# A conditioned transformer block on one core: moving a softmax division to another slot, and spreading the softmax maxima in 32-column tiles

## The chip, the core and the metric

The kernel runs on one core of one Trainium2 chip. A core has TensorE (PE in the profile; PEld is its weight load), VectorE (DVE), ScalarE (ACT), GpSimd (POOL) and SyncE (SP, which here only issues DMAs). The metric is device time in microseconds (us): of the kernel before, 2452.37 us as the median of three runs (2448.12 to 2452.83). Times of single instructions come from one profiled execution.

## What is computed

x is [4, 1024, 512] and t is [4, 128], both f32. The block is added to x once more at the end.

```python
def _tc_rmsnorm(x, t, gw, gb, bw, bb):
    g = (t @ gw.T + gb)[:, None, :]
    b = (t @ bw.T + bb)[:, None, :]
    inv_rms = jax.lax.rsqrt(jnp.mean(x * x, axis=-1, keepdims=True) + EPS)
    return g * x * inv_rms + b

def _attention(x, Wq, Wk, Wv, Wo):          # 16 heads of 32
    attn = jnp.einsum('blhd,bmhd->bhlm', q, k) / scale
    p = jax.nn.softmax(attn, axis=-1)
    o = jnp.einsum('bhlm,bmhd->blhd', p, v).reshape(B, L, D)
    return o @ Wo.T

def _swiglu(x, gate_w, hid_w, out_w):       # hidden width 2048
    return jax.nn.silu(x @ gate_w.T) * (x @ hid_w.T) @ out_w.T

y = x + _attention(_tc_rmsnorm(x, t, g1w, g1b, b1w, b1b), Wq, Wk, Wv, Wo)
return x + y + _swiglu(_tc_rmsnorm(y, t, g2w, g2b, b2w, b2b), gate_w, hid_w, out_w)
```

## The kernel before

**Tiling.** Features lie on the partitions. The 4096 tokens form 8 blocks of 512. Attention is cut into units j: one block, four heads, 256 queries; there are 64 of them. A unit takes four rounds g, each with 256 of the 1024 keys, so there are 256 rounds of attention. Four rounds from a multiple of 4 are called a group here, and the rounds in it slot 0 to slot 3 (in the code: kind = g % 4). Eight groups are the 32 rounds of a block; "position 12" means the group whose first round has g % 32 = 12.

**A round.** Round g multiplies the scores of its keys (`scores`, L310), copies them from PSUM to SBUF (`keep`, L317, on ACT) and takes a running maximum on DVE (`running_max`, L322 and L325). After the fourth round of a unit the maximum is taken over the keys: eight PE transposes (`max_T`, L331, in slot 0), then DVE (`parts`, L337 to L342), which writes each negated maximum as three bf16 numbers whose sum is the f32 value: 4 heads by 3 parts, 12 columns of a 128-column tile `split`. In slot 1, `parts_T` transposes these on PE into 12 rows (L347) and ACT copies them to `mT` (L349); `spread` multiplies `mT` with 0/1 weights `select` (L357), which adds the three parts and repeats the sum on all 128 partitions, two heads at a time; ACT copies the result to `shift` (L358). Then, five rounds after its scores, a tile gets its maximum subtracted on DVE (`shifted`, L363) and goes through the exponential on ACT (`exponential`, L366). One round later `weighted` multiplies it with v on PE (av, L376), and a DMA from POOL adds it to the unit's running sum (`accumulate`, L390). When a unit is through, DVE folds the sum in two (`fold_sum`, L398, slot 0), PE sums it over the keys (`sums`, L408), ACT copies that (L413), DVE takes the reciprocal (`inverse`, L416) and multiplies it with the copied av (`normalize`, L425) into oT. The last two are the division that the change moves. oT is read by the output projection of the block, more than a group later.

**What lies around it.** In the opening, rounds 0 to 59, PE also projects keys, queries and values of all batches from a queue of chains. From round FS = 60 on, the feed-forward part of earlier blocks fills PE: each pair of rounds handles one 128-wide slice p of the hidden layer, by a scheme that shares products (pa and pb, in eighths called pair_15 to pair_7), with DVE steps L546 (`sub_5`), L524 (`add_15`, which pa<-x,fa of the next even round needs), L561 (`gate`), L564 (`hidden`), and the contraction pc, which DVE adds to the result (`take_contract`, L577). Norms are spread over fixed rounds too: L632 (a reciprocal of 128x512) and L193 (scaling) for the next batch in the opening; L138, L193, L491 to L497 at positions 8 to 28 of a block later.

**Order.** The order of instructions on PE, DVE, ACT and POOL is the order of the code, written out by hand; semaphores come from the tile framework. So an instruction that waits holds up everything behind it on its engine. Helper `mm` (L103) splits a matmul into pieces of columns[0] output rows: 32 (four pieces, each on its own 32 columns of PE's array, shown as 128*32) in nearly all work, 128 in parts of the opening and at its start. Forms as 128*32 give the rows times the columns of the array that an instruction uses. PSUM tiles of tag "w" come from two banks that pc, pt, both sp and pa take in turn.

Of the kernel before, what the change touches and what calls it, by code (L numbers as in the profile page):

```python
# [11 lines left out]
BF16 = mybir.dt.bfloat16  # L12
# [5 lines left out]
P = 128  # L18
# [6 lines left out]
def tile_cond_transformer_block(  # L25
# [13 lines left out]
    nc = tc.nc  # L39
# [7 lines left out]
    DH = D // N_HEADS  # L47
    HG = P // DH
    FG = 4
    HQ = 256  # L50
# [6 lines left out]
    const = ctx.enter_context(tc.tile_pool(name="const", bufs=1))  # L57
    sb = ctx.enter_context(tc.tile_pool(name="sb", bufs=1))
# [8 lines left out]
    ident_bf = const.tile([P, P], BF16, tag="ident_bf", name="ident_bf")  # L67
# [8 lines left out]
    NP = 3 * HG  # L76
    split = [const.tile([P, QT, P], BF16, tag=f"split{i}", name=f"split{i}") for i in range(2)]
# [2 lines left out]

    pick = const.tile([NP, HG], F32, tag="pick", name="pick")
    nc.vector.tensor_reduce(pick, ident[:NP, :NP].rearrange("p (h i) -> p h i", i=3), AX.X, ALU.add)
    select = const.tile([NP, HG, P], BF16, tag="select", name="select")
    nc.vector.tensor_copy(select, pick.unsqueeze(2).to_broadcast([NP, HG, P]))
    mod = const.tile([P, 4 * C, B], F32, tag="mod", name="mod")

    condT = const.tile([P, B], F32, tag="condT", name="condT")
# [15 lines left out]
    def mm(dst, w, moving, start: bool, stop: bool, seeded: bool = False):  # L103
        n = columns[0]
        for k in range(0, P, n):
            nc.tensor.matmul(  # L106
                dst[k : k + n, :], w[:, k : k + n], moving, start=start, stop=stop, skip_group_check=seeded
            )

    y, wkq, wv, wo, kq, v = {}, {}, {}, {}, {}, {}  # L110
    raw, rmax, shift, mT, av, acc, avs, oT = {}, {}, {}, {}, {}, {}, {}, {}
# [232 lines left out]
    def parts_T(j: int):  # L344
        pt = ps.tile([P, HQ // P, P], BF16, tag="w", name=f"pt{j}")
        for qt in range(HQ // P):
            nc.tensor.transpose(pt[:, qt, :], split[j % 2][:, qt, :], ident_bf)  # L347
        mT[j] = sb.tile([NP, HQ], BF16, tag="mT", name=f"mT{j}", bufs=2)
        nc.scalar.copy(mT[j], pt[:NP, :, :].rearrange("p a b -> p (a b)"))  # L349

    def spread(j: int, k: int):

        if k == 0:
            shift[j] = sb.tile([P, HG, HQ], F32, tag="shift", name=f"shift{j}")
        pp = ps.tile([P, 2, HQ], F32, tag="w", name=f"sp{j}_{k}")
        for i in range(2):
            nc.tensor.matmul(pp[:, i, :], select[:, k + i, :], mT[j], start=True, stop=True)  # L357
        nc.scalar.copy(shift[j][:, k : k + 2, :], pp)  # L358

    def shifted(r: int, heads: slice = slice(0, HG)):  # L360
# [54 lines left out]
    def inverse(j: int):  # L415
        nc.vector.reciprocal(state["total", j], state["total", j])  # L416

    def normalize(j: int):

        m, qh = divmod(j, NB // HQ)  # L420
        n, hg = divmod(m, C)
        total = state.pop(("total", j))
        if (n, hg) not in oT:
            oT[n, hg] = sb.tile([P, NB], F32, tag=f"oT{hg}", name=f"oT{m}")
        nc.vector.tensor_tensor(oT[n, hg][:, qh * HQ : (qh + 1) * HQ], avs.pop(j), total, ALU.mult)  # L425
# [157 lines left out]
    GB = C * (NB // HQ)  # L583
    BS = GB * UN
# [38 lines left out]
    for b in range(1, B):  # L623
        for half in range(QB):
            s = math.ceil((len(queue) + 1) / PACE)
            s4 = s - 4 - (s - 6) % UN
            tag = f"a{b}_{half}"
# [10 lines left out]
    FS = BS + 28  # L638
# [3 lines left out]
    for n in range(NBLK):  # L642
# [7 lines left out]
        if n < NBLK - 1:  # L650
            tag = f"f{n}"
# [46 lines left out]
    with tc.manual_schedule(  # L698
# [35 lines left out]
        direct = NR // UN - 2  # L734
        late = None
        g = 0
# [31 lines left out]
        while g < END:  # L768
            kind = g % UN
# [6 lines left out]
            j_n = g // UN - 3  # L776
            n_on = 0 <= j_n < NR // UN
            ffn = g >= FS
            p = (g - FS) // 2
# [3 lines left out]
            if kind == 1 and m_on:  # L783
                parts_T(j_m)
            if g < NR:
                scores(g)
            if kind == 1 and m_on:
                spread(j_m, 0)
# [14 lines left out]
            if kind == 1 and m_on:  # L803
                spread(j_m, 2)
                mT.pop(j_m)
                shifted(r_x, slice(0, HG // 2))
                shifted(r_x, slice(HG // 2, HG))
# [54 lines left out]
            else:  # L862
# [34 lines left out]
                    chain(g)()  # L897
                for fn, a in halfway.pop(g, []):
                    fn(*a)
            if kind == 0 and n_on and j_n < direct:  # L900
                inverse(j_n)

                if j_n != GB:
                    normalize(j_n)
            columns[0] = DH
            for fn, a in ended.pop(g, []):
                fn(*a)
# [93 lines left out]
```

## Time and profile before

| What | us |
|---|---|
| median of three runs | 2452.37 |
| the profiled execution, in all | 2447.08 |
| its span, first to last instruction | 2445.3 |
| PE / DVE / ACT / POOL busy | 2386.7 / 1938.9 / 1416.2 / 172.8 |
| 256 exponentials, mean of one (L366) | 1.915 |
| 256 score copies, mean of one (L317) | 1.873 |
| 192 shifts in one piece, mean of one (L363) | 2.282 |
| 64 reciprocals of a division (L416) | 1.744 |
| 64 products of a division (L425) | 0.425 |
| 256 spread matmuls (L357) | 0.270 |
| 128 transposes of the parts (L347) | 0.219 |

Busy time counts an engine's instructions, not what it waited for; matmuls overlap, so their single durations can't be added. The opening takes the first 540 us, the rounds with feed-forward work run to about 2125 us, the feed-forward rest to the end. A line of the timeline gives the start in us from the span's start, the time in us (of several instructions merged, from the first's start to the last's end), engine, line, operation, what it writes and reads, the form, the count, and in brackets the idle time before it and what ended that. A line of the waits gives who waited for whom, the total in us, the number and the longest. A line of windows gives the stretch, its length, busy time and count of PE, PEld, DVE, ACT and POOL, then the granted PE clock (1.00 is full), the DMA engines' busy share and GB/s.

### The profile page before, as it was taken

To read this page: it belongs to the slowest core of one execution; us is meant where nothing else is said; L and a number is where in the kernel's file an instruction comes from. 1 tells how busy PE (TensorE), PEld (TensorE's weight loads), DVE (VectorE), ACT (ScalarE), POOL (GpSimd) and SP (SyncE) were. 2 spreads that over 40 slices of the span, in tenths; PEclk is the share of its full clock that TensorE was granted. 3 is DMA by queue.
4 is the path that set the end of the run, shared out by engine and by line. 5 is a ranking of instruction groups with operands and counts; after the bars stand their busy time and mean duration, and the time that the engine had idled before them with its cause. 6 is when DMAs were issued, how large, how long until landed. Compare 5 with 4: busy or idle time off the path is not lost. (4 is left out here: it accounts for less than half of the span.)

```text
span 2445.3 us, 71149 instructions
## 1 busy us (share of the span) xinstructions
PE 2386.7 (98%) x31785; PEld 1128.7 (46%) x31785; DVE 1938.9 (79%) x2180; ACT 1416.2 (58%) x1495; POOL 172.8 (7%) x207
## 2 busy tenths in 40 slices
PE   8999999999999999999999999999999999999999
PEld 3333333334445544545454544454455445444544
DVE  2688888878889988999799979997999889843332
ACT  3677777666566655666566656665666566512110
POOL 0000000000000000000000000000000000000000
PEclk9999999999999999999999999999999999999999
DMA  6599999988888988889788988888888888853442
GB/s 214 168 284 253 250 256 235 232 205 216 206 201 208 220 224 197 208 215 234 195 208 208 237 206 197 209 226 211 206 205 206 226 200 205 212 165 118 143 129 71
DMA packets 185983, 501.70 MB, mean 205 GB/s; under 512 B 21319, under 2 KB 78663, under 8 KB 158286
## 3 DMA queue, kind: packets, MB, share of 16 engines
q0 software_dynamic: 28656, 208.68, 44.2%
q1 hardware_dynamic: 156734, 288.47, 35.5%
q8 instruction: 250, 4.10, 0.7%
q14 instruction: 55, 0.45, 0.1%
q10 hardware_dynamic: 288, 0.01, 0.0%
HBM read 246.44 MB, written 41.97 MB: 118 GB/s over the span
## 5 line engine op out<-in xcount | busy, mean ns | idle before, releaser
L317 ACT COPY raw<-sc 128x2048 f32<-128x2048 f32 x256 | 479.4, 1873 | 200.1 <-PE sc L310 133.4
L363 DVE TENSOR_TENSOR raw<-raw,shift 128x2048 f32<-128x2048 f32 (+1 forms) x320 | 589.0, 1856 | 3.3 <-ACT shift L358 2.8
L366 ACT ACTIVATE raw<-raw 128x2048 f32<-128x2048 f32 x256 | 490.2, 1915 | 128.9 <-DVE raw L363 124.8
L322 DVE TENSOR_TENSOR rmax<-rmax,raw 128x1024 f32<-128x1024 f32 x384 | 469.5, 1223 | 54.4 <-ACT raw L317 47.9
L106 PE MATMUL pc<-h,ow 128*32 128x512 f32 x4096 | 467.7, 593 | 3.3 <-DMA ow<-in_out_w 2.3
L376 PE MATMUL av<-raw,v 128*32 128x256 f32 x4096 | 275.8, 387 | 34.5 <-ACT raw L366 30.6
L390 POOL DMA_DIRECT2D raw<-raw x192 | 165.7, 863 | 1959.3 <-ACT raw L366 886.0
L310 PE MATMUL sc<-q,k 32*128 32x256 f32 x4096 | 293.3, 400 | 0.3 <-ACT raw L317 0.3
L106 PE MATMUL pa<-x,fa 128*32 128x256 f32 x4096 | 268.2, 379 | 0.3 <-DVE pa L524 0.2
L106 PE MATMUL pa<-sums,fw 128*32 128x256 f32 x4096 | 267.9, 379 | 0.0
L106 PEld LDWEIGHTS pc<-h,ow 128*32 128x32 f32 x4096 | 128.2, 110 | 246.7 <-issue 225.4
L310 PEld LDWEIGHTS sc<-q,k 32*128 32x128 f32 x4096 | 184.9, 184 | 116.6 <-issue 66.6
L106 PE MATMUL pkq<-y,wkq 128*32 128x512 f32 (+1 forms) x1664 | 234.3, 601 | 4.2 <-ACT y L196 4.1
L376 PEld LDWEIGHTS av<-raw,v 128*32 128x32 f32 x4096 | 107.4, 109 | 159.0 <-ACT raw L366 52.2
L106 PEld LDWEIGHTS pa<-x,fa 128*32 128x32 f32 x4096 | 131.1, 110 | 103.0 <-issue 8.8
L106 PEld LDWEIGHTS pa<-sums,fw 128*32 128x32 f32 x4096 | 133.1, 110 | 87.9
L577 DVE SCALAR_TENSOR_TENSOR res<-pc,res 128x512 f32<-128x512 f32 x128 | 88.2, 689 | 76.0 <-PE pc L106 75.0
L556 ACT ACTIVATE t<-pa 128x512 f32<-128x512 f32 x128 | 77.5, 605 | 109.9 <-PE pa L106 109.5
L539 ACT COPY pb<-pa 128x256 f32<-128x256 f32 x128 | 45.9, 359 | 160.3 <-PE pa L106 158.9
L106 PE MATMUL pb<-x,fw 128*32 128x256 f32 x2048 | 134.0, 379 | 1.2 <-ACT pb L539 1.2
L106 PE MATMUL pa<-x,fw 128*32 128x256 f32 x2048 | 135.2, 381 | 0.0
L106 PEld LDWEIGHTS pkq<-y,wkq 128*32 128x32 f32 (+1 forms) x1664 | 73.2, 118 | 131.5 <-issue 118.3
(106 smaller groups left out, 2214.4 us busy)
## 6 DMA issues: line engine op xcount, KB each, us to landing
raw<-raw POOLq DMA_DIRECT2D x192, 1024.0 KB, 9.1
fw<-sw SPq DMA_DIRECT2D x128, 512.0 KB, 7.5
fa<-in_gh_w SPq DMA_DIRECT2D x128, 384.0 KB, 6.5
ow<-in_out_w SPq DMA_DIRECT2D x128, 256.0 KB, 3.7
wkq<-in_kq_w SPq DMA_DIRECT2D x32, 512.0 KB, 5.9
v<-vs SPq DMA_DIRECT2D x128, 128.0 KB, 5.5
k<-kqs SPq DMA_DIRECT2D x124, 128.0 KB, 6.8
kqs<-st SPq DMA_DIRECT2D x61, 256.0 KB, 7.4
```

Of the source, the lines that this page charges most:

```text
L106: nc.tensor.matmul(dst[k : k + n, :], w[:, k : k + n], moving, start=start, stop=stop, skip_group_check=seeded)
L310: nc.tensor.matmul(sc[:, i, k, :], keys[rows, k * P : (k + 1) * P], queries[rows, :], start=True, stop=True)
L317: nc.scalar.copy(raw[r].rearrange("p k h q -> p h k q"), state.pop(("sc", r)))
L322: nc.vector.tensor_tensor(rmax[j], rmax[j], raw[r][:, k, :, :], ALU.max)
L363: nc.vector.tensor_tensor(t, t, s.unsqueeze(1).to_broadcast(list(t.shape)), ALU.add)
L366: nc.scalar.activation(raw[r], raw[r], AF.Exp)
L376: nc.tensor.matmul(av[j][i * DH : (i + 1) * DH, :], v[m, u][:, k, i * DH : (i + 1) * DH], raw[r][:, k, i, :], start=(kt == 0), stop=(kt == ...
L390: nc.gpsimd.dma_start(out=acc[j].rearrange("p k h q -> p (k h q)"), in_=raw[r].rearrange("p k h q -> p (k h q)"), accum_op=ALU.add,)
L539: nc.scalar.copy(bank_b[p][:, RIGHT], bank_a[p][:, RIGHT])
L556: nc.scalar.activation(state["t", p], bank_a[p], AF.Tanh, scale=0.5)
L577: nc.vector.scalar_tensor_tensor(r, pp, 0.5, r, ALU.mult, ALU.add)
```

## The change

Two parts. The first is in the spread: `select` gets 128 rows instead of 12 (the others zero), `mT` becomes two constant tiles of 128 rows, zeroed once and of which the copy writes the first 12; the transposes take 32 columns of `split` instead of 128, and the spread goes through `mm`. Since columns[0] is 32 there, each of the four spread matmuls of a unit becomes four of 32 columns. The sums are the same, with zeros added.

The second moves the division (L416, L425) of most units. Before, it is the last DVE work of slot 0 but for the work listed to come after a round. Now it stays there only for the last unit of each block, and from round 60 on for positions 0, 4, 8, 16 and 20; at positions 12, 24 and 28 and in the opening it comes at the same place in slot 2, two rounds later. The conditions on j_n == GB and direct are as before.

```diff
-    select = const.tile([NP, HG, P], BF16, tag="select", name="select")
-    nc.vector.tensor_copy(select, pick.unsqueeze(2).to_broadcast([NP, HG, P]))
+    select = const.tile([P, HG, P], BF16, tag="select", name="select")
+    nc.vector.memset(select, 0.0)
+    nc.vector.tensor_copy(select[:NP], pick.unsqueeze(2).to_broadcast([NP, HG, P]))
+    parts_of = [const.tile([P, HQ], BF16, tag=f"mT{i}", name=f"mT{i}") for i in range(2)]
+    for t in parts_of:
+        nc.vector.memset(t, 0.0)
...
-            nc.tensor.transpose(pt[:, qt, :], split[j % 2][:, qt, :], ident_bf)
-        mT[j] = sb.tile([NP, HQ], BF16, tag="mT", name=f"mT{j}", bufs=2)
-        nc.scalar.copy(mT[j], pt[:NP, :, :].rearrange("p a b -> p (a b)"))
+            nc.tensor.transpose(pt[:DH, qt, :], split[j % 2][:, qt, :DH], ident_bf)
+        mT[j] = parts_of[j % 2]
+        nc.scalar.copy(mT[j][:NP], pt[:NP, :, :].rearrange("p a b -> p (a b)"))
...
-            nc.tensor.matmul(pp[:, i, :], select[:, k + i, :], mT[j], start=True, stop=True)
+            mm(pp[:, i, :], select[:, k + i, :], mT[j], True, True)
...
-            if kind == 0 and n_on and j_n < direct:
-                inverse(j_n)
-
-                if j_n != GB:
-                    normalize(j_n)
+            if n_on and j_n < direct and kind in (0, 2):
+
+
+                at = g - kind
+                in_first = j_n % GB == GB - 1 or (at >= FS and at % BS not in (12, 24, 28))
+                if in_first == (kind == 0):
+                    inverse(j_n)
+
+                    if j_n != GB:
+                        normalize(j_n)
```

## The prediction

> **What bounds the kernel now.** I read the page's shares of busy time, then the list of waits, then the timeline of one ordinary group of four rounds, of one opening group and of one group with norm work.
>
> ```profile
> PE 2386.7 (98%) x31785; PEld 1128.7 (46%) x31785; DVE 1938.9 (79%) x2180; ACT 1416.2 (58%) x1495; POOL 172.8 (7%) x207
> ...
> PE av L376 <- ACT raw L366: 30.6, 24, 3.5
> ...
> 1516.30 1.05 PE L106 MATMUL pb<-x,fw 128*32 128x256 f32 x16
> ...
> 1517.27 0.12 PEld L347 LDWEIGHTS <-split 128*128 128x128 bf16 x2 [0.41 <-DVE res L577]
> 1517.29 0.27 PE L347 MATMUL pt<-ident_bf,split 128*128 128x128 bf16 x2
> 1517.49 1.15 PE L310 MATMUL sc<-q,k 32*128 32x256 f32 x16
> 1518.46 0.38 PE L357 MATMUL sp<-mT,select 12*128 12x256 bf16 x2
> 1518.77 1.07 PE L376 MATMUL av<-raw,v 128*32 128x256 f32 x16
> 1519.77 0.39 PE L357 MATMUL sp<-mT,select 12*128 12x256 bf16 x2
> 1520.09 1.07 PE L106 MATMUL pa<-x,fw 128*32 128x256 f32 x16
> 1520.20 0.59 ACT L358 COPY shift<-sp 128x512 f32<-128x512 f32 x1 [0.68 <-PE sp L357]
> 1520.68 1.88 ACT L317 COPY raw<-sc 128x2048 f32<-128x2048 f32 x1
> 1522.44 0.39 ACT L402 COPY avs<-av 128x256 f32<-128x256 f32 x1
> 1522.70 1.94 ACT L366 ACTIVATE raw<-raw 128x2048 f32<-128x2048 f32 x1
> 1523.68 1.15 PE L310 MATMUL sc<-q,k 32*128 32x256 f32 x16
> ```
>
> PE is the bound. Where it stops, it waits almost always for one thing: in slot 2 of a group, av waits for an exponential, whose shift DVE did late. Adding up the timeline's gaps before av, about 17.5 us of the 30.6 lie in the opening (rounds 6 to 59) and nearly all the rest in later groups, 1.28 us at position 16 and 0.67 at position 24 of each 32-round block. (Position 12 waits 0.55, put down to another ACT copy behind the same exponential.) In the ordinary group shown no wait is reported, but there is little room: the exponential ends at 1524.64 and av starts at 1524.76. Its chain is spread copy, score copy, avs copy, exponential: ACT, without a gap, not DVE.
>
> **What the Trainium skill says.** "TensorEngine Tiling (Array Packing)", section Key Properties: changing the tiling mode drains the array, changing the tile inside a mode doesn't. The trace agrees: av to its 128*32 successor takes 0.89 us from start to start, av to the 12*128 spread 1.00. The same page, Gotcha 2, says that column tiling excludes fast weight load; no row here shows bf16 in column tiles. "TensorE: Matmul & The Clock Gate", Part 1: an idle array falls to half clock and needs about 3.4 us of work to recover. The trace shows three such falls, after the stalls at 160, 227 and 361 us:
>
> ```profile
> 160.00:164.00 4.00, 3.87 (x32) 1.42 (x36) 3.97 (x4) 3.56 (x4) 0.00 (x0) 0.65 0.94 219
> 227.00:231.00 4.00, 4.00 (x32) 1.26 (x28) 3.94 (x7) 2.01 (x2) 0.00 (x0) 0.59 0.98 289
> 361.00:366.00 5.00, 4.95 (x40) 1.67 (x44) 4.97 (x5) 4.16 (x4) 0.11 (x1) 0.68 0.98 317
> ```
>
> The column after POOL is the granted clock: 4.00 x 0.35 + 4.00 x 0.41 + 5.00 x 0.32 = 4.6 us lost.
>
> **Part A, the tile mode.** Per group, four full-width bf16 matmuls become sixteen 32-column ones. In the f32 rows four column tiles run side by side (starts 7 ns apart, the next four 216 ns later), at the same rate per column as full-width f32. A full-width spread matmul occupies 107 to 113 ns. So four narrow bf16 ones should take 107 ns together; bounds: 107 below, 216 (the f32 figure) above. I take 107.
> First spread: scores to spread had no switch (0.97), spread to av 0.31; now one switch comes before it instead of after: 1.28 becomes 1.30. Second spread: 1.00 + 0.32, then 0.89, becomes about 0.86 + 0.22 + 0.86. Part of this is lost, since its PSUM bank and the one for the next pa are released by the two ACT copies of the spread: from score start to score start 6.19 becomes 5.98, a gain of 0.20 us. The transposes save a switch of 0.11 too, but gain nothing: the row above has them waiting for L577 to release the bank (ends 1517.24, transpose 1517.27). In the opening they follow a 128*128 projection, so there a switch is added: 14 x 0.04 = 0.6 us lost.
> In an ordinary group the gain isn't all kept. ACT's chain starts at the second spread, which comes only 0.10 earlier against the scores; with the 0.12 of room, of which 0.05 stays as the signal's delay, av comes 0.16 earlier. Eighteen groups at positions 0, 4, 20: 2.8 us. Six at 8, which PE alone bounds (av 7 us after its exponential): 0.20 each, 1.2. Six at 16, ACT-bound through a table load: 0.085 each, 0.5. Sum 4.5, less 0.6 = 3.9 us. The new memsets (three of about 0.17 to 0.2 us) lie in the 21 us that DVE waits for the first norm.
>
> **Part B in the opening.** Reciprocal and product take 1.74 + 0.42 (2.13 start to start) and leave the end of slot 0 in eleven groups. The clearest:
>
> ```profile
> 148.99 1.75 DVE L416 RECIPROCAL total<-total 128x256 f32<-128x256 f32 x1
> 150.77 0.42 DVE L425 TENSOR_TENSOR oT<-avs,total 128x256 f32<-128x256 f32 x1
> 151.12 3.34 DVE L632 RECIPROCAL tota<-tota 128x512 f32<-128x512 f32 x1
> 155.79 2.35 DVE L363 TENSOR_TENSOR raw<-raw,shift 128x1024 f32<-128x1024 f32 x2
> 158.17 1.91 ACT L366 ACTIVATE raw<-raw 128x2048 f32<-128x2048 f32 x1 [3.48 <-DVE raw L363]
> 160.13 1.94 PE L376 MATMUL av<-raw,v 128*32 128x256 f32 x16 [3.46 <-ACT raw L366]
> ```
>
> DVE is continuous from the division to the shift, so av comes 2.13 earlier. Group by group, each capped by its stall and by ACT's copies: rounds 14 and 38 2.13 each, 22 2.0, 30 2.07, 26 0.4, the groups of 44 and 48 together 1.4, and 0.1 to 0.15 at six more (part A's share): 11.0 us. The division comes back at the end of slot 2, ahead of the next shift. Where that round's exponential waits for the score copy anyway (14, 22, 38, 50, 54) it is hidden. Where DVE is the later one, av of the next slot 0 had 0.9 to 1.4 us of room and is late by 0.6 (18), 0.7 (30), 0.6 (34): 1.9 us; 46's is in the 1.4. Net 9.1. With stalls of at most 1.4 us left I expect all three clock falls gone (bounds: none to all): stalls of 1.5 and 1.6 us elsewhere in the opening caused none. That is 4.6; I take 4.5.
>
> **Part B later.** Positions 12, 24, 28 move too.
>
> ```profile
> 1562.56 0.68 DVE L577 SCALAR_TENSOR_TENSOR res<-pc,res 128x512 f32<-128x512 f32 x1
> 1563.16 0.42 DVE L546 TENSOR_TENSOR pb<-pb,p 128x256 f32<-128x256 f32 x1
> 1563.49 0.68 DVE L493 TENSOR_TENSOR sums<-x,sums 128x512 f32<-128x512 f32 x1
> 1564.09 2.29 DVE L363 TENSOR_TENSOR raw<-raw,shift 128x2048 f32<-128x2048 f32 x1
> 1566.29 1.22 DVE L322 TENSOR_TENSOR rmax<-rmax,raw 128x1024 f32<-128x1024 f32 x1
> ...
> 1569.16 0.43 DVE L524 TENSOR_TENSOR pa<-pa,p 128x256 f32<-128x256 f32 x1
> ```
>
> Position 24: without the division slot 2's av comes 0.9 earlier (then ACT's chain ends last), so 1.2 of the 2.13 becomes idle DVE. In slot 2 the division enters between L546 and L493, in a stretch with no idle DVE time, and everything down to L524 is 2.13 later; L524's consumer, pa<-x,fa at 1569.74, had 0.15 of room. Walking the rows on to round 189, with part A in it: 1.1 us lost. Position 28: 0.3 gained, and in slot 2, with 1.1 of room, 0.8 lost: 0.5 lost. Position 12: 0.55 of stall and part A's 0.20 gained, 0.73 lost: nothing. Six blocks: 6 x 1.1 = 6.7; seven groups at 28: 3.4. Sum 10.1 lost.
>
> **Sum.** 3.9 + 9.1 + 4.5 - 10.1 = 7.4 us gained. The profiled execution took 2447.1 us (span 2445.3), 5.3 under the median of the runs, 2452.4; I take the difference off the median: 2445.0.
>
> **Rivals.** (1) The third slot has room: the shift's successors don't bind, the moved division costs nothing anywhere. Then the 1.9 and the losses fall away, and positions 12, 24, 28 gain 0.75, 0.9, 0.3: 3.9 + 11.0 + 4.5 + 12 = 31 us, 2421. For it: DVE idles 21% in all. Against: the rows above have none to spare just there. (2) Slower: narrow bf16 matmuls run at the f32 tiles' 216 ns per four instead of 107. Each of the 63 groups then has four sets costing 0.107 more on PE and in ACT's chain, 27 us: 2472. It decides once a set takes over about 135 ns. For it: no fast weight load, and no row shows the form; against: f32 tiles lose nothing to full width. (3) Position 24's new stall (about 1.6 us in one piece) drops the clock, as the 2.0 us one at 227 did: 6 x 1.7 = 10 us, 2455. (4) The opening keeps its time: its 16 DMA engines are shown at about 0.95 to 1.1 busy around the stalls, so loads may end last once DVE doesn't; the 9.1 shrink to about 2: 2452. Against: no PE wait in the opening is put down to a DMA.
>
> **Chances.** Forecast 0.50, rivals 0.15, 0.12, 0.10, 0.13. A measurement here can tell about 0.2% (4.9 us) from no change. The forecast's own spread, some 6 us either way, crosses that in a tenth to a fifth of its share. Faster 0.59, same 0.22, slower 0.19. Range 2420 to 2457: rival 1 at the low end, rival 3 at the high one, rival 2 left out.
>
> **What would show it.** Right: spread matmuls 128*32 with sets about 107 to 120 ns apart; second spread to next pa 0.22; ordinary groups about 0.15 us shorter; no half clock before 540 us; av stalls of rounds 22 and 30 gone, of 14 and 38 near 1.4; in each block new waits of PE for L524 and the exponential around rounds 28 and 0. Wrong: sets 216 apart, groups longer; or slot 0 after a moved division without a wait.

## The result and the profile after

The changed kernel takes 2449.38 us (median; 2447.45 to 2455.29), the kernel before, run beside it, 2451.79 (2446.14 to 2453.66): ratio 0.9995, 95% interval 0.9986 to 1.0004, so between 3.4 us won and 1.0 lost. By these runs the change can't be told apart from no change. The profiled execution of the changed kernel took 2455.29 us (span 2453.4) and was the longest of its runs; that of the kernel before was 4.7 us under its median. So the two spans, 8.1 us apart the wrong way round, may be compared stage by stage, not as sums. All line numbers grow by 6 (L376 is now L382), and the spread goes through `mm`, L112.

The page's first part and the list of waits of the changed kernel (who waited for whom: total us, times, longest):

```profile
PE 2385.5 (97%) x32553; PEld 1135.9 (46%) x32553; DVE 1940.7 (79%) x2183; ACT 1413.2 (58%) x1495; POOL 172.4 (7%) x207
```
```profile
PE av L382 <- ACT raw L372: 35.1, 37, 1.6
...
PE pc L112 <- DMA ow<-in_out_w: 4.2, 1, 4.2
...
PE pa L112 <- DVE pa L530: 4.1, 21, 0.2
```

The wait of av for the exponential has not shrunk, it has grown from 30.6 to 35.1 us; the longest single one fell from 3.5 to 1.6. The wait of pa for L530 (L524 before) was one of 0.2 us and is 21 now, together 4.1. To see where this lies I take the start of the first score matmul of each group of four rounds and subtract:

| stage, us | before | after |
|---|---|---|
| start to round 60 | 539.87 | 526.99 |
| rounds 60 to 71 | 92.14 | 96.92 |
| rounds 72 to 251 | 1448.58 | 1458.92 |
| round 252 to the end | 364.72 | 370.53 |

The opening won 12.9 us and everything after it gave 21 back (in this execution). Here is the opening at the place that the prediction showed, round 14, in the timeline after:

```profile
153.46 2.35 DVE L369 TENSOR_TENSOR raw<-raw,shift 128x1024 f32<-128x1024 f32 x2
...
155.09 1.15 PE L316 MATMUL sc<-q,k 32*128 32x256 f32 x16
...
155.85 1.91 ACT L372 ACTIVATE raw<-raw 128x2048 f32<-128x2048 f32 x1 [1.43 <-DVE raw L369]
157.81 0.59 PEld L382 LDWEIGHTS av<-raw,v 128*32 128x32 f32 x16 [1.98 <-ACT raw L372]
157.81 1.07 PE L382 MATMUL av<-raw,v 128*32 128x256 f32 x16 [1.57 <-ACT raw L372]
```

The stall before av is 1.57 us where it was 3.46. And the windows of the same stretches as before have their granted clock (the column after POOL) at full; between 22 and 595 us this trace has no half clock at all:

```profile
150.00:160.00 10.00, 8.43 (x119) 3.42 (x115) 9.93 (x10) 7.87 (x8) 0.86 (x1) 1.00 1.04 301
...
220.00:230.00 10.00, 9.90 (x109) 3.74 (x109) 9.85 (x13) 7.35 (x7) 0.86 (x1) 1.00 1.04 297
...
360.00:370.00 10.00, 10.00 (x124) 3.90 (x120) 9.90 (x11) 7.61 (x7) 0.86 (x1) 1.00 1.02 300
```

The ordinary group (position 20, slot 1) after, the same place as in the prediction:

```profile
1516.16 0.27 PE L353 MATMUL pt<-ident_bf,split 128*32 128x128 bf16 x2
...
1516.37 1.15 PE L316 MATMUL sc<-q,k 32*128 32x256 f32 x16
...
1517.44 0.40 PE L112 MATMUL sp<-mT,select 128*32 128x256 bf16 x8
...
1517.67 1.04 PE L382 MATMUL av<-raw,v 128*32 128x256 f32 x16
1517.95 0.58 ACT L364 COPY shift<-sp 128x512 f32<-128x512 f32 x1 [1.12 <-PE sp L112]
...
1518.59 0.40 PE L112 MATMUL sp<-mT,select 128*32 128x256 bf16 x8
...
1518.80 1.05 PE L112 MATMUL pa<-x,fw 128*32 128x256 f32 x16
...
1519.04 0.58 ACT L364 COPY shift<-sp 128x512 f32<-128x512 f32 x1 [0.50 <-PE sp L112]
...
1519.67 0.59 PEld L112 LDWEIGHTS pa<-x,fa 128*32 128x32 f32 x16 [0.30 <-ACT shift L364]
...
1522.40 1.15 PE L316 MATMUL sc<-q,k 32*128 32x256 f32 x16
```

Eight narrow spread matmuls hold PE for 0.21 to 0.23 us (1517.44 to 1517.67, 1518.59 to 1518.80), two sets of four at 107 to 120 ns, as taken. Score to score is 6.03 us (1516.37 to 1522.40), not 5.98. The ACT rows show why: the second spread (1518.59) begins when the first copy has ended (1517.95 + 0.58 = 1518.53), and pa<-x,fa (1519.67) when the second has (1519.62).

Last, rounds 187 and 188, where position 24's division arrives:

```profile
1561.09 0.42 DVE L552 TENSOR_TENSOR pb<-pb,p 128x256 f32<-128x256 f32 x1
...
1561.42 1.74 DVE L422 RECIPROCAL total<-total 128x256 f32<-128x256 f32 x1
...
1563.20 0.42 DVE L431 TENSOR_TENSOR oT<-avs,total 128x256 f32<-128x256 f32 x1
...
1563.54 0.69 DVE L499 TENSOR_TENSOR sums<-x,sums 128x512 f32<-128x512 f32 x1
...
1564.14 2.28 DVE L369 TENSOR_TENSOR raw<-raw,shift 128x2048 f32<-128x2048 f32 x1
...
1566.46 1.91 ACT L372 ACTIVATE raw<-raw 128x2048 f32<-128x2048 f32 x1 [2.61 <-DVE raw L369]
...
1568.42 1.07 PE L382 MATMUL av<-raw,v 128*32 128x256 f32 x16 [1.57 <-ACT raw L372]
...
1569.69 1.07 PE L112 MATMUL pa<-x,fa 128*32 128x256 f32 x16 [0.20 <-DVE pa L530]
```

DVE has no gap from the division to the shift, nor from there to L530; ACT stands 2.61 us and PE 1.57, then 0.20 more for L530.

### The profile page after: what moved, and what is told of

It reads as the page before. It is cut to its first block, busy times and chain, and to the rows that moved or that the text cites. A ratio compares the mean times of both kernels' runs of the same rounds, so it can differ in the third digit from the quotient of the medians.

```text
span 2453.4 us, 72677 instructions
## 1 busy us (share of the span) xinstructions
PE 2385.5 (97%) x32553; PEld 1135.9 (46%) x32553; DVE 1940.7 (79%) x2183; ACT 1413.2 (58%) x1495; POOL 172.4 (7%) x207
## 5 line engine op out<-in xcount | busy, mean ns | idle before, releaser
L112 PE MATMUL pc<-h,ow 128*32 128x512 f32 x4096 | 470.5, 596 | 5.2 <-DMA ow<-in_out_w 4.2
L382 PE MATMUL av<-raw,v 128*32 128x256 f32 x4096 | 271.9, 383 | 35.6 <-ACT raw L372 35.1
L112 PE MATMUL pa<-x,fa 128*32 128x256 f32 x4096 | 272.5, 384 | 4.1 <-DVE pa L530 4.1
L112 PE MATMUL pa<-sums,fw 128*32 128x256 f32 x4096 | 271.5, 383 | 0.0
L112 PEld LDWEIGHTS pc<-h,ow 128*32 128x32 f32 x4096 | 128.6, 110 | 250.7 <-issue 231.9
L112 PE MATMUL pkq<-y,wkq 128*32 128x512 f32 (+1 forms) x1664 | 232.5, 594 | 4.3 <-ACT y L202 4.1
L112 PEld LDWEIGHTS pa<-x,fa 128*32 128x32 f32 x4096 | 124.7, 110 | 119.7 <-DVE pa L530 21.4
L382 PEld LDWEIGHTS av<-raw,v 128*32 128x32 f32 x4096 | 110.4, 109 | 149.4 <-ACT raw L372 66.0
L112 PEld LDWEIGHTS pa<-sums,fw 128*32 128x32 f32 x4096 | 134.4, 111 | 90.0 <-issue 3.4
L112 PE MATMUL pb<-x,fw 128*32 128x256 f32 x2048 | 134.0, 379 | 1.2 <-ACT pb L545 1.2
L112 PE MATMUL pa<-x,fw 128*32 128x256 f32 x2048 | 134.0, 379 | 0.0
L552 DVE TENSOR_TENSOR pb<-pb,p 128x256 f32<-128x256 f32 x128 | 55.0, 430 | 99.8 <-PE pb L112 94.2
```

The costliest lines, as they stand in the source:

```text
L112: nc.tensor.matmul(dst[k : k + n, :], w[:, k : k + n], moving, start=start, stop=stop, skip_group_check=seeded)
L382: nc.tensor.matmul(av[j][i * DH : (i + 1) * DH, :], v[m, u][:, k, i * DH : (i + 1) * DH], raw[r][:, k, i, :], start=(kt == 0), stop=(kt == ...
L552: nc.vector.tensor_tensor(b[:, LEFT], b[:, RIGHT], fifth.pop(p), ALU.subtract)
```

## The experiments

Lengths of a group by its position, in us, from the traces. From round 72 on the figures repeat to within 0.1 from block to block; the few groups with a clock fall, or another single hold-up of up to 0.4, are left out.

| position | before | spread only | division only | opening only | after |
|---|---|---|---|---|---|
| 0 | 29.73 | 29.63 | 30.54 | 29.63 | 30.51 |
| 4 | 29.73 | 29.63 | 29.73 | 29.63 | 29.63 |
| 8 | 43.82 | 43.79 | 43.82 | 43.79 | 43.79 |
| 12 | 31.41 | 31.41 | 30.79 | 31.41 | 30.70 |
| 16 | 31.07 | 31.04 | 31.87 | 31.04 | 31.84 |
| 20 | 29.73 | 29.63 | 29.73 | 29.63 | 29.63 |
| 24 | 30.47 | 30.47 | 29.73 | 30.47 | 29.63 |
| 28 | 30.43 | 30.43 | 32.35 | 30.43 | 32.32 |
| round 60 starts at | 539.87 | 536.79 | 527.91 | 527.31 | 526.99 |

**Spread only.** The changed kernel with the division where it was.

```diff
-            if n_on and j_n < direct and kind in (0, 2):
...
+            if kind == 0 and n_on and j_n < direct:
+                inverse(j_n)
```


> The tile mode alone, every division in slot 0 as before. Theory (the tile mode is worth little, since ACT's chain behind the second spread ends last): 0.10 us at 18 groups, 0.09 at 6, 0.03 at 6, nothing where norm work stalls, so 2 to 3 us, about 2449. Rival (PE is the bound, so the 0.16 us that a group's PE work shrinks by is kept in all 63): 10 us, about 2442.

2446.40 us beside 2450.39 of the kernel before; ratio 0.9985 (0.9976 to 0.9994). The column says how little comes from the later groups: 0.10 each at 0, 4 and 20, 0.03 at 8 and at 16. 3.1 us of the gain is in the opening, where two clock falls are left of three; the granted clock below full is in these windows:

```profile
160.00:170.00 10.00, 10.00 (x89) 3.16 (x84) 8.51 (x8) 5.92 (x7) 0.86 (x1) 0.83 1.03 263
350.00:360.00 10.00, 6.31 (x68) 2.28 (x64) 9.93 (x10) 6.45 (x7) 0.86 (x1) 0.89 1.04 296
360.00:370.00 10.00, 10.00 (x104) 3.36 (x100) 7.86 (x8) 6.17 (x7) 0.86 (x1) 0.94 0.97 232
```

The two falls follow the stalls of rounds 14 and 38, both 3.69 us here. Round 22 stalled for 2.22 us, longer than the 1.99 before, and no fall followed; the round is 1.47 us shorter for it. Another 1.35 us lies before round 0, whose start varies from 49.55 to 51.30 us over the kernels here. These two make up nearly all of the 3.1 us, so the tile mode itself won next to nothing in the opening, and its own worth is the 2 us or so of the later groups.

**Division only.** The kernel before, with the change's condition for the division and the old spread.

```diff
-            if kind == 0 and n_on and j_n < direct:
...
+            if n_on and j_n < direct and kind in (0, 2):
...
+                in_first = j_n % GB == GB - 1 or (at >= FS and at % BS not in (12, 24, 28))
```


> The division moved as in the change, the spread as before. Theory: about 12 us gained by round 60, then some 1.9 us lost in each of six blocks at positions 12, 24 and 28: about 2452, no change. Rival (the tile mode is what shortened the opening): no gain by round 60, about 2462.

2453.09 us; ratio 1.0014 (1.0004 to 1.0023), by its interval slower than before. Round 60 starts at 527.91: 12.0 of the opening's 12.9 us are there with the division alone moved. And the losses at 28, 0 and 16 are all there without the tile mode.

**Opening only and later only.** The changed kernel, with the division moved in the rounds before 60 alone, and in the later ones alone:

```diff
-                in_first = j_n % GB == GB - 1 or (at >= FS and at % BS not in (12, 24, 28))
+                in_first = j_n % GB == GB - 1 or at >= FS
```
```diff
-                in_first = j_n % GB == GB - 1 or (at >= FS and at % BS not in (12, 24, 28))
+                in_first = j_n % GB == GB - 1 or (at < FS or at % BS not in (12, 24, 28))
```


> Tile mode as in the change, the division moved in the opening alone. Theory (the moves at positions 12, 24, 28 cost about what the opening gains): 12.9 us gained by round 60 and 2 to 3 more after it, about 2437, some 12 us faster than the change. Rival (those moves are neutral, and what was lost after round 60 came from the longer wait for the first output weights and from falls of the clock): like the change, about 2449.

> Tile mode as in the change, the division moved at positions 12, 24 and 28 from round 60 on, and in slot 0 in the opening. Theory: the opening as before, then 1.6 to 2.7 us lost per block: about 2461. Rival (those moves are neutral): about 2450.

Opening only: 2437.08 us, ratio 0.9938 (0.9923 to 0.9953). Later only: 2460.31 us, 1.0041 (1.0027 to 1.0055). The two halves of the move have opposite signs, and their intervals lie apart, on two sides of 1. Later only has the changed kernel's group lengths to 0.02 at all positions from round 72 on, clock falls aside. Opening only beats both kernels; 2449.38 - 2437.08 = 12.3 us is what the later moves cost the changed kernel (the two were timed in separate comparisons; by their ratios it is 14 us). In the table it is 2.02 us a block (12: -0.71, 16: +0.80, 24: -0.84, 28: +1.89, 0: +0.88), six blocks, 12.1 us. In the later groups av stalls where it did before, and a little longer, as PE's work ahead of it is shorter: 0.64 us at position 12 (0.55 before), 1.39 at 16 (1.28), 0.82 at 24 (0.67). The list of waits, over the whole span, has:

```profile
PE av L382 <- ACT raw L372: 27.3, 31, 1.6
...
PE sum L414 <- DVE raw L404: 4.2, 1, 4.2
...
PE av L382 <- ACT totf L157: 3.8, 6, 0.6
PE pc L112 <- DMA ow<-in_out_w: 2.5, 1, 2.5
```

Timed once more beside the last experiment below:

> The kernel with only the opening moved, timed once more, as its first comparison rests on few runs: both theories 0.993 to 0.995 of the kernel before, about 2437 us.

2435.06 us, ratio 0.9939 (0.9928 to 0.9951), the same again.

**Why do the later moves cost: the length of the work, or its place?** (In the expectations that follow, the "second slots" of the first are those with kind == 2, the slots of arrival; the "fourth slot" of the next is slot 3; the "second slot" of the one with the small copy is slot 1.)

```diff
-    def inverse(j: int):
-        nc.vector.reciprocal(state["total", j], state["total", j])
+    def inverse(j: int, n: int = HQ):
+        t = state["total", j][:, :n]
+        nc.vector.reciprocal(t, t)
...
-                    inverse(j_n)
+                    inverse(j_n, HQ // 2 if at >= FS and kind == 2 else HQ)
```


> The changed kernel, but in the second slots from round 60 on the reciprocal is taken of 128 of the 256 columns only, so half of the divisors there stay uninverted; the instruction should fall from 1.74 to about 0.9 us on VectorE, everything else stays. Theory (VectorE has no time free between its last needed result and the shift of the third slot, so each microsecond put there is paid for): the groups of position 28 go from 32.32 to about 31.5 us, of position 0 from 30.51 to about 29.65, of position 16 from 31.84 to about 31.05. Rival (what costs is that the block of work stands in another slot, with its semaphores and buffers, not its length): the three lengths stay within 0.1 us.

So half of those divisors stay as they are, and the times show only what the length of the instruction does. The smallest of this line in the trace is 941 ns, with 128 columns, beside 1743 ns with 256, so the moved work is 0.80 us shorter:

```profile
L423 DVE RECIPROCAL total<-total x64: 941/1743/1752, 164.6 to 2149.1; 128x256 f32<-128x256 f32 x45, 128x128 f32<-128x128 f32 x19
```

Position 28 went from 32.32 to 31.52, position 0 from 30.51 to 29.71, position 16 from 31.84 to 31.04. All three by 0.80: each microsecond that the division has too much there is paid in full. (2431.56 us in its one run.)

**Which wait holds it.** The same division, in the same later groups, further down DVE's queue: behind the shift that the exponential waits for.

```diff
+            if kind == 3 and n_on and j_n < direct and g - 3 >= FS and (g - 3) % BS in (12, 24, 28):
+                inverse(j_n)
+                normalize(j_n)
...
-                if in_first == (kind == 0):
+                if in_first == (kind == 0) and (in_first or at < FS):
```


> The changed kernel, but from round 60 on the moved division (positions 12, 24, 28) is issued in the third... fourth slot of its group directly after the shift that the exponential needs, instead of in the slot before that shift. Theory (VectorE's whole queue is full there: the first output projection's addition binds about as closely as the exponential): the waits of av for the exponential vanish, waits of the projection's next product for the addition take over, and the groups of positions 28, 0 and 16 stay near 32.3, 30.5 and 31.8 us. Rival (only the shift and the exponential were late): 30.4, 29.6 and 31.0 us, and about 2437 us for the whole.

Groups of 32.32, 30.51 and 31.84 us (2450.61 us in its one run): not 0.01 us of the loss is saved. The timeline of round 188 shows another wait in the place of the first, and the list of waits has the totals:

```profile
1562.12 1.07 PE L382 MATMUL av<-raw,v 128*32 128x256 f32 x16
...
1564.55 0.43 DVE L530 TENSOR_TENSOR pa<-pa,p 128x256 f32<-128x256 f32 x1
1565.03 0.59 PEld L112 LDWEIGHTS pa<-x,fa 128*32 128x32 f32 x16 [2.33 <-DVE pa L530]
1565.04 1.07 PE L112 MATMUL pa<-x,fa 128*32 128x256 f32 x16 [1.84 <-DVE pa L530]
```
```profile
PE av L382 <- ACT raw L372: 21.1, 18, 1.6
PE pa L112 <- DVE pa L530: 19.8, 19, 1.8
```

The stall of av is gone, and pa waits 1.84 us where av waited 1.57 and pa 0.20. L530 comes after the division in both orders, and it binds as closely as the exponential. Moving the division behind the shift, but still ahead of L530, had nothing to win here. Behind L530 it was not tried.

**The three moves one by one.** In blocks two to seven (counted from zero) only position 12, 24, 28, 12, 24, 28 moves.

```diff
-                in_first = j_n % GB == GB - 1 or (at >= FS and at % BS not in (12, 24, 28))
+                in_first = j_n % GB == GB - 1 or (at >= FS and at % BS != (0, 0, 12, 24, 28, 12, 24, 28)[at // BS % 8])
```


> The changed kernel with the opening moved as it is, but after round 60 only one position of each block moves: 12, 24, 28, 12, 24, 28 in blocks two to seven. It parts the three moves. Theory (the place where it leaves gains what its wait was, the place where it arrives loses): position 12 moved alone: its group 31.41 to 30.70, the next 31.04 to 31.84, together a loss of 0.1 us; position 24 alone: 30.47 to 29.63 and then 30.43 to about 32.3, a loss of about 1.0; position 28 alone: the group of 28 near 30.2 and the next 29.63 to 30.51, a loss of 0.5 to 0.9. Rival (the moves make each other late, as position 28 has both an arrival and a departure in it): each alone costs under 0.3 us.

| moved alone | group it leaves | next group | together | blocks |
|---|---|---|---|---|
| position 12 | 31.41 to 30.70 | 31.04 to 31.83 | +0.08 | second |
| position 12 | 31.41 to 30.70 | 31.04 to 32.20 | +0.45 | fifth |
| position 24 | 30.47 to 29.63 | 30.43 to 32.56 | +1.29 | third and sixth |
| position 28 | 30.43 to 30.20 | 29.63 to 30.52 | +0.66 | fourth |

The run took 2441.17 us, once. The fifth block's next group had a longer stall of av, 0.64 us beside 0.27 in the second. In the trace DVE's L552 started 0.37 us later there, after 0.61 us without work instead of 0.24, while PE's rows just before it are the same in both blocks; what held it isn't shown. With all three moved, position 16 took 31.84 in each of the six blocks, so I take the second block's value. Then each move costs by itself what it costs among the others: 0.08 + 1.29 + 0.66 = 2.03, and 2.02 with all three. They don't make each other late.

**What ends last in the ordinary group.** Opening only, plus one small copy on ACT ahead of the exponential of slot 1:

```diff
+    spare_tile = const.tile([P, 8], F32, tag="spare_tile", name="spare_tile")
...
+                if g >= FS and g % BS in (1, 5, 21):
+                    nc.scalar.copy(spare_tile, ones_sum[:, :8])
```


> The kernel with only the opening moved, plus one small extra copy (128x8) on ScalarE after the av products in the second slot of positions 0, 4 and 20 from round 60 on; its result is used nowhere. Theory (in the ordinary groups ScalarE's chain of score copy, shift copy and exponential ends last, so what the tile mode shortens on TensorE counts only where it brings that chain forward): the groups of positions 0, 4 and 20 grow by about the copy's own duration, 0.2 us. Rival (TensorE's own work sets these groups): they stay at 29.63 us.

The groups took 29.72 instead of 29.63 (2435.63 us in its one run), less than expected. The timelines say why. First this kernel, then opening only (its lines are one lower):

```profile
1254.30 0.39 ACT L409 COPY avs<-av 128x256 f32<-128x256 f32 x1
...
1254.56 0.22 ACT L820 COPY spare_tile<-ones_sum 128x8 f32<-128x8 f32 x1
1254.66 1.93 ACT L373 ACTIVATE raw<-raw 128x2048 f32<-128x2048 f32 x1
```
```profile
1252.45 0.38 ACT L408 COPY avs<-av 128x256 f32<-128x256 f32 x1
...
1252.71 1.93 ACT L372 ACTIVATE raw<-raw 128x2048 f32<-128x2048 f32 x1
```

The copy lasts 0.22 us but the next instruction starts 0.10 after it; avs to exponential is 0.36 us instead of 0.26. What ACT is held for, 0.10, comes out as 0.09 in the group. So ACT's chain does end last; PE gains from shorter matmuls only what reaches that chain.

**A load that is late.** In round 68 PE waits for the first output weights of the feed-forward part (`load_ow`), 1.8 to 4.2 us in the profiles that put this wait down to the load. It has nothing to do with the change but blurs its measurement. Opening only, with that load three rounds earlier:

```diff
-            if g == FS + 2 * FG - 2:
+            if g == FS + 2 * FG - 5:
```


> The kernel with only the opening moved, and the load of the first output weights of the feed-forward part (the first of its kind) issued three rounds earlier, in round 63 instead of 66. So far PE waited 2.0 to 4.2 us for it in round 68, with or without a clock fall after. Theory (the load is late because it is issued late, behind other transfers): the wait goes, the group of rounds 68 to 71 takes about 29.7 us in place of 32.2 to 36.7, and the median is 2 to 4 us below the kernel without this. Rival (its time comes from the traffic of that stage, which will delay the next load as well): the wait turns up at the second load, or other transfers get later, and the group keeps at least 2 us of it.

2430.44 us (2429.61 to 2436.02), ratio 0.9928 (0.9915 to 0.9941), beside 2435.06 for opening only on the same chip. The two intervals overlap, so the times alone don't part them; the stage does. The windows over it, opening only (its second timing) first:

```profile
580.00:600.00 20.00, 16.78 (x220) 8.23 (x216) 13.42 (x16) 9.63 (x10) 1.72 (x2) 0.85 0.91 247
```
```profile
580.00:600.00 20.00, 20.00 (x306) 10.57 (x302) 17.91 (x22) 11.83 (x12) 1.72 (x2) 1.00 0.90 228
```

The wait (3.2 us in that run) and the clock fall behind it are gone, and rounds 68 to 71 take 29.63 us instead of 35.83. The load was issued at 545.8 us instead of 581.2; how long it took isn't in this trace. No wait for a later load has come in its place. This is the fastest version that was run with the whole computation.

## Why the prediction came out as it did

The time came out inside the range, 4.4 us above the forecast of 2445.0, and the likeliest case, a gain that can be measured, did not: 7.4 us were forecast and 2.4 measured (-1.0 to 3.4). The range was 37 us wide, so to lie in it says little; the terms say more.

**Opening: right in sum, 13.0 forecast and 12.9 measured.** From division only, against before: rounds 14 and 38 gained 3.4 and 3.7 us, of which 2.13 is the division and the rest, 1.3 and 1.5, the clock; 22 gained 3.75 (2.0 and 1.75); 30 gained 2.07 (2.07 forecast), 26 0.34 (0.4), 44 to 51 together 1.2 (1.4). The clock falls gone are 1.3 + 1.75 + 1.5 = 4.6 (4.5). The losses at the next slot 0 were 0.61, 0.68 and 0.61 (0.6, 0.7, 0.6). One was missed: the division of round 22 was called hidden, and round 24 lost 0.67. It was about made up by the tile mode, for which 0.6 had been put down as lost: after starts round 60 another 0.9 us before division only, 0.36 of it in place before round 0. And there is luck in the 4.6: that the stall of round 22 drops the clock at all is a matter of the execution. Spread only and later only, with the division still in slot 0, stalled there for 2.22 and 2.21 us and kept the clock, and so did the kernel before itself in round 30, after 2.00 us. Beside such an execution the opening wins some 1.75 us less.

**Part A later: the mechanism right, the size twice too large.** 4.5 us forecast, 18 x 0.10 + 6 x 0.03 + 6 x 0.03 = 2.2 measured. The sets took 107 to 120 ns, as taken, and the second spread is followed by pa after 0.22, as forecast. The term that failed is "ACT's chain starts at the second spread, which comes only 0.10 earlier against the scores". Measured from the scores, the second copy of the spread starts after 2.67 us (1519.04 - 1516.37) and started after 2.71 (1520.20 - 1517.49): 0.04. With the 0.07 of room (0.12 less 0.05) av comes 0.11 earlier, 7.16 us after the scores instead of 7.27, where 0.16 was forecast; the group gains 0.10. The first spread comes 0.10 later than before, since the switch of mode now stands ahead of it (1.07 after the scores, was 0.97), and its copy now holds the second spread back, where before the av products did (1519.77, when the copy had ended at 1519.52). The page "TensorEngine Tiling (Array Packing)", section Key Properties, on which the count of switches rested, agrees with the rows; which wait takes over when a switch is gone is not in it, and was in the rows. Position 8 was said to be bound by PE alone and gained 0.03 of 0.20: in its round 9 PE waits 0.11 us before the output projection, and the trace names the copy avs (L408), on the same ACT chain, as what ended that wait. What a change to that copy would win was not tried.

**Part B later: the mechanism right, 10.1 forecast and about 12 measured.** Position 24 alone loses 1.29 (1.1 forecast), 28 alone 0.66 (0.5), 12 alone 0.08 (0). The forecast gains at the places left were close (0.9 and 0.3; measured 0.84 and 0.23); the larger part of the error is in the arrivals: 2.13 at 28 (2.0), 0.89 at 0 (0.8). With position 24 moved alone the whole start-to-start length of reciprocal and product, 2.13 us, was paid. The forecast's reason, no idle DVE time down to L530, held in the stronger form that half a reciprocal and the order behind the shift have shown.

**Rivals.** That slot 2 has room falls with the three groups that shrank by exactly the 0.80 us taken from the reciprocal. Sets at 216 ns fall with the rows. That the opening keeps its time falls with round 60. The clock at position 24's new stall came in part: in the profile of the changed kernel it fell in four of six blocks, 3.41 us at half clock each, and the group was 33.36 instead of 32.32 us, 1.04 more (1.7 had been taken). In division only, the same stalls of 1.50 us brought no fall in six blocks; in later only, of 1.56 or 1.57, one in six. So the length of the stall alone doesn't decide it (the last section has what more the traces show), and the forecast was right to keep it apart from its sum.

**The sum.** 12.9 + 2.2 - 12.1 = 3.0 us gained, and 2.4 was measured by the medians. That the profiled spans differ by 8.1 us the other way has these causes besides: three clock falls (3.1 us) in rounds 72 to 251, round 68's late load (36.69 us for its group instead of 32.09), and the end, which varies from 364.7 to 371.6 us over all kernels here, from round 252 on.

## What to carry to other kernels

Moving work from a slot is two edits with two prices: read the stall that it leaves and the slack where it arrives, stage by stage, and take each stage for itself; here one condition on the round number parted a gain of 12.6 us (round 60 at 539.87 and 527.31, opening only) from 12 us of loss. When an engine's queue is full up to two results that are due together, changing their order moves the wait from one reader to the other and not the time. A switch or a stall that is removed on the busiest engine is worth only what the next chain, here two copies on ACT, leaves of it.

## What was not expected of the hardware

- The clock fell after stalls of PE of about 1.6 us, but not after each: four in six, one in six, none in six, for nearly equal stalls. "TensorE: Matmul & The Clock Gate", Part 1, speaks of idle gaps above about 3.4 us; the measured stalls are shorter, and the measurement decides. The 3.41 us of one fall agree with the page's window, and so does its remark that the window runs freely: in the changed kernel the falls start at 793.57, 1052.98, 1827.80 and 2087.22 us, 76, 227 and 76 times 3.413 us apart, and in each of the twelve traces all changes of the clock lie on one such grid, to 0.005 us. So it should matter how much of a stall lies in one window of the grid. Here are three of these windows from the changed kernel, each with all or most of a stall of 1.57 us in it, the first with a fall behind it, the other two without:

```profile
790.15:793.57 3.42, 1.65 (x32) 0.60 (x28) 3.42 (x6) 3.33 (x3) 0.57 (x1) 1.00 0.96 251
1308.98:1312.39 3.41, 1.82 (x32) 0.91 (x36) 3.41 (x6) 3.37 (x3) 0.86 (x1) 1.00 0.73 263
1564.98:1568.39 3.41, 1.87 (x32) 0.95 (x24) 3.41 (x4) 1.93 (x2) 0.00 (x0) 1.00 0.99 170
```

PE idles 1.77 us in the first, with the 0.20 for L530 in it, and 1.59 and 1.54 in the others. Over all traces, from 100 to 2110 us: all 11 windows of the grid in which PE idled for 60% or more had a fall behind them, none under 51% had one, and of the 15 between, 9 had. The share of idle time in a window goes far to tell a fall, but its bound isn't sharp by this measure.

- An ACT copy of 128x8 shows 0.22 us and holds the engine for 0.10.
- The first load of output weights was waited for until 11.9 to 13.9 us after its issue (13.6 in the second timing of opening only, 581.2 to 594.8). Its landing itself isn't in the traces; of its kind, 23 of 128 loads have one, at a median of 3.0 to 3.7 us and at most 15.1.
